# Gate and up's tiles 8 and 9: the fourth block product by seven products in half-width banks instead of by two plain ones

## The chip, the cores and the metric

The kernel runs on one core of one Trainium2 chip. The metric is the device time of one execution in microseconds; lower is better. The profile comes from one further execution, with TensorE (PE), its weight loads (PEld), VectorE (DVE), ScalarE (ACT), GpSimd (POOL) and SyncE (SP, which issues most transfers) recorded apart.

## The reference, cut to what matters

```python
xn = _layernorm(x, axis=-1)                       # x: 8 x 1024 x 512, f32
s = _L0_attn_ref(xn, Wq, Wk, Wv, Wo, Wg, decay_logits, out_scale)
# _L0_ffn_ref, with INTER = 1376 rows of gate and up, weights looked up in a table of 16
gate = einsum('bsh,oh->bso', xn, lut[gate_idx])
up = einsum('bsh,oh->bso', xn, lut[up_idx])
h = silu(gate) * up
ffn = einsum('bsh,oh->bso', h, lut[down_idx])
x = x + s * silu(ffn)
```

The change touches only `gate` and `up`, for 256 of the 1376 rows (tiles 8 and 9 of 128 rows each; tile 10 has the 96 left over).

## The kernel before, in words

A first phase does the attention for all eight batch entries (bodies) and builds the weights of the feed-forward part, which it writes to DRAM. A second phase does gate, up and down body by body, 1024 tokens each. All in float32. `keep_order` pins the instructions of TensorE, VectorE, ScalarE and GpSimd to the order in which the program was traced, so that each engine's queue is what the code says, line after line.

Gate and up are computed by a Strassen-like scheme on two levels. On the outer level, a 2 x 2 block product is done by seven block products, named by the keys 1 to 7. Of each tile's weights the blocks and their sums lie in `W_OF` order, of x in `X_OF` order. On the inner level, each block product is again done by seven products, by the same scheme, for which x has seven halves of columns (`H` = 256 tokens) in `D_OF` order; `sums_of_x` makes them in place, so that one raw quarter of x is overwritten and has to be fetched again by `restore` before the raw blocks are used.

A `Node` is one step of the inner level. It holds four PSUM banks of 512 columns, in the roles s11, s12, s21 and sE, of which there are two each, and has two halves, `a` = 0 and 1, each of 256 columns. Its seven products each issue two matmuls of 256 columns, one per half:

- `first`: product 1 into s11, and ScalarE copies s11 to s12 (L794).
- `fifth` and `fifth_copy`: product 5 into sE, and ScalarE copies it to `e` in SBUF (L801).
- `sixth`: product 6 onto s12; ScalarE copies s12 to s21 (L805); VectorE adds `e` to s12 (L806).
- product 2 onto s11. Then s11 is complete: quarter 0.
- `seventh`: product 7 onto s21; VectorE writes s21 + `e` to sE (L810), which is quarter 3.
- product 3 onto s12 (quarter 1), and product 4 onto s21 (quarter 2).

As a quarter gets complete, the step's `empty(t, n)` brings it out of PSUM. The loop in `quads` interleaves two nodes: the following node's product 1 goes between the node's products 2 and 7, and the following node's product 5 between products 3 and 4.

For the tiles 0 to 7 a node's two halves are two pairs of tiles with one key (`steps(q)` for q = 0 and 1, of `NQ` = 2). For the one pair left, tiles 8 and 9 (q = `NQ`), the two halves are two keys: (1, 6), (5, 7), (2, 3), by `pair_steps`. `node_23` ends with two VectorE additions (L924, L926) and two silus on ScalarE (L925, L927) for each quarter. Key 4 is left over. It is done by the class `Fourth`: each of the two tiles has one product of 512 columns by the plain scheme, of two matmuls (L826) from the raw blocks of x, which VectorE adds to `u3` (L835). `Fourth` stands in the loop as the following of node (2, 3): its first product lies between that node's products 2 and 7, its second between products 3 and 4. After it, `after_23` multiplies both halves of h by u3 and e5 on GpSimd (L936).

Next comes, in the bodies 1 to 7, tile 10 by `single` (the tail o = 10, seven products of two 512-column matmuls, L731, from raw blocks of x); in body 0 that tile was done ahead of the quads. Then `down` runs with its own nodes (`DownNode`, L1037 to L1075; its copies are L1059, L1066 and L1070).

Weights come through `ring`, three slots, one per node, `Fourth` or tail; SP issues a node's load as soon as the slot of three nodes earlier is free.

The restores of x are issued from ScalarE's queue (L853): (4) by the last node of quad 1, and after that (1, 6), (5, 7) and (2, 3) by the pair's nodes.

Of the kernel before, what the change touches and what calls it, by code (L numbers as in the profile page):

```python
# [9 lines left out]
F32 = mybir.dt.float32  # L10
# [4 lines left out]
ALU = mybir.AluOpType  # L15
AX = mybir.AxisListType

P = 128
# [30 lines left out]
def recurrent_block(ctx: ExitStack, tc, x, wq, wk, wv, wo, wg, decay_logits, out_scale, lut, gidx, uidx, didx, out):  # L49
# [19 lines left out]
    nc = tc.nc  # L69
# [5 lines left out]
    U = 512  # L75
# [5 lines left out]
    NK = (NO - 1) // 2  # L81
# [164 lines left out]
    def ffn_weights(build, pool, pair_pool):  # L246
# [9 lines left out]
        def gate_up(o):  # L256
            s, m = OCH[o]
            n = 2 * NV * m
            idx = build.tile([P, NB], I32, name="idx", tag="idx", bufs=2)
            iv = idx[:, :n].rearrange("p (a b) -> p a b", b=m)  # L260
            gs, us = (src[:, s : s + m].rearrange("(c p) b -> p c b", p=P) for src in (gidx, uidx))
            nc.sync.dma_start(out=iv[:, 2:6, :], in_=gs)
            nc.sync.dma_start(out=iv[:, 0:2, :], in_=us[:, 0:2, :])
            nc.sync.dma_start(out=iv[:, 6:8, :], in_=us[:, 2:4, :])
            yield
            wf = pool.tile([P, 2 * NB], F32, name="wgu", tag="wgu", bufs=2)
            yield from look_up(build, wf[:, :n], idx[:, :n], P, n)
            w = wf[:, : 2 * n].rearrange("p (k two m) -> p k two m", two=2, m=m)
            a21, a11, a12, a22, s1, s2, s3, s4 = (w[:, k] for k in range(8))
            nc.gpsimd.tensor_tensor(s1, a21, a22, ALU.add)  # L270
            nc.gpsimd.tensor_tensor(s2, s1, a11, ALU.subtract)
            yield
            nc.gpsimd.tensor_tensor(s3, a11, a21, ALU.subtract)
            nc.gpsimd.tensor_tensor(s4, a12, s2, ALU.subtract)
            wide = wf[:, 2 * m : 2 * n].rearrange("p (a b) -> p a b", b=m)
            if o >= 4 * NQ:
                defer(3, lambda: nc.sync.dma_start(out=wgu_d[o], in_=wide))
            if o >= 2 * NK:
                return
            if o % 2 == 0:  # L280
                upper.append(w[:, 1:])
                return
            up, low = upper.pop(), w[:, 1:]
            to = quad_d[o // 4][:, :, o // 2 % 2, :].rearrange("p k (t m) -> p k t m", m=P)
            pair = pair_pool.tile([P, 7, 4, P], F32, name="pair", tag="pair")
            nc.sync.dma_start(out=to[:, :, 0:2, :], in_=up)
            defer(3, lambda: nc.sync.dma_start(out=to[:, :, 2, :], in_=low[:, :, 1, :]))
            b21, b22, b11, b12 = low[:, :, 0], low[:, :, 1], up[:, :, 0], up[:, :, 1]
            nc.gpsimd.tensor_tensor(pair[:, :, 0], b21, b22, ALU.add)
            yield  # L290
            nc.gpsimd.tensor_tensor(pair[:, :, 1], pair[:, :, 0], b11, ALU.subtract)
            yield
            nc.gpsimd.tensor_tensor(pair[:, :, 2], b11, b21, ALU.subtract)
            yield
            nc.gpsimd.tensor_tensor(pair[:, :, 3], b12, pair[:, :, 1], ALU.subtract)
            defer(4, lambda: nc.sync.dma_start(out=to[:, :, 3:7, :], in_=pair))
            for _ in range(3):
                yield
# [383 lines left out]
    def phase_2():  # L682
        with (
# [12 lines left out]
            def bank(role, name):  # L696
                return psp.tile([P, U], F32, name=name, tag=role)
# [62 lines left out]
            class Node:  # L760
# [2 lines left out]

                def __init__(self, b, q, ks, xs):
                    self.ks, self.xs = ks, xs

                    self.restores = ks if q == NQ else (4,) if (q, ks) == (NQ - 1, (4, 4)) else ()
                    name = f"{b}_{q}_{ks[0]}"  # L770
                    self.w = ring.tile([P, 2, 7, P], F32, name=f"wq{name}", tag="wr")
                    w = self.w.rearrange("p a t m -> p a (t m)")
                    if q < NQ:
                        nc.sync.dma_start(out=w, in_=quad_d[q][:, W_OF[ks[0]], :, :])
                    else:
                        for a, k in enumerate(ks):
                            nc.sync.dma_start(out=w[:, a, :], in_=quad_d[q][:, W_OF[k], 0, :])
                    self.t = [bank(r, f"{r}{name}") for r in ("s11", "s12", "s21", "sE")]
                    self.name = f"e{name}"

                def product(self, n, i, start=False):
                    for a in range(2):
                        nc.tensor.matmul(  # L783
                            self.t[n][:, ts(a, H)],
                            lhsT=self.w[:, a, (0, 1, 6, 2, 3, 4, 5)[i - 1], :],
                            rhs=self.xs[:, X_OF[self.ks[a]], D_OF[i], :],
                            start=start and a == 0,
                            stop=False,
                            skip_group_check=True,
                        )  # L790

                def first(self):
                    self.product(0, 1, True)
                    nc.scalar.copy(self.t[1], self.t[0])  # L794

                def fifth(self):
                    self.product(3, 5, True)
                    self.e = tmp.tile([P, U], F32, name=self.name, tag="e")

                def fifth_copy(self):  # L800
                    nc.scalar.copy(self.e, self.t[3])  # L801
# [6 lines left out]
                def seventh(self):  # L808
                    self.product(2, 7)
                    nc.vector.tensor_tensor(self.t[3], self.t[2], self.e, ALU.add)  # L810

            class Fourth:


                def __init__(self, b, xs, u3):
                    self.b, self.xs, self.u3 = b, xs, u3
                    self.w = ring.tile([P, 14, P], F32, name=f"w4{b}", tag="wr")
                    for r in range(2):
                        nc.sync.dma_start(
                            out=self.w[:, ts(r, 2), :], in_=wgu_d[4 * NQ + r][:, ts(W_OF[4], 2), :]  # L820
                        )

                def product(self, r, role):
                    ps = bank(role, f"{role}{self.b}_4_{r}")
                    for n in range(2):
                        nc.tensor.matmul(  # L826
                            ps,
                            lhsT=self.w[:, 2 * r + n, :],
                            rhs=self.xs[:, X_OF[4], ts(n, 2), :],
                            start=n == 0,  # L830
                            stop=n == 1,
                            skip_group_check=True,
                        )
                    o = self.u3[:, ts(r, 2), :]
                    return lambda: nc.vector.tensor_tensor(o, ps.rearrange("p (a t) -> p a t", a=2), o, ALU.add)  # L835

                def first(self):
                    self.product(0, "s11")()

                def fifth(self):  # L840
                    self.add = self.product(1, "sE")

                def fifth_copy(self):
                    self.add()

            def quads(b, xs, h, sums, at_last):

# [53 lines left out]
                def pair_steps():  # L901
# [2 lines left out]
                        (t[:, :, :H], t[:, :, H:])  # L904
                        for t in (tmp.tile([P, 4, U], F32, name=f"{k}{b}_l", tag=k) for k in ("p1", "u2"))
                    )
                    room[0] = u3

                    def of_h(half, n):
                        r, c = divmod(n, 2)  # L910
                        t = half * U + c * H
                        return h[:, 4 * NQ + r, t : t + H]
# [10 lines left out]
                    def node_23(t, n):  # L923
# [2 lines left out]
                        nc.vector.tensor_tensor(of_h(1, n), t[n][:, H:], u2[:, n], ALU.add)  # L926
                        nc.scalar.activation(of_h(1, n), of_h(1, n), AF.Silu)  # L927

                    def after_57():
                        for n in (0, 3, 1, 2):  # L930
                            nc.gpsimd.tensor_tensor(e5[:, n], e5[:, n], u3[:, n], ALU.add)

                    def after_23():
                        for half, other in ((0, u3), (1, e5)):
                            for n in (0, 3, 1, 2):
                                nc.gpsimd.tensor_tensor(of_h(half, n), of_h(half, n), other[:, n], ALU.mult)  # L936

                    yield (1, 6), node_16, None
                    yield (5, 7), node_57, after_57
                    yield (2, 3), node_23, after_23  # L940

                room = [None]
                def every():
                    for q in range(NQ):
                        for ks, empty, after in steps(q):
                            yield Node(b, q, ks, xs), empty, after
                    for ks, empty, after in pair_steps():
                        yield Node(b, NQ, ks, xs), empty, after
                    yield Fourth(b, xs, room[0]), None, None
                    yield None, None, None  # L950

                todo = every()
# [381 lines left out]
```

## Time and profile before

| | us |
|---|---|
| median of 3 runs | 2119.15 (2118.79 to 2119.32) |
| profiled execution, its time | 2119.36 |
| its span, first to last instruction | 2117.6 |
| TensorE busy | 2109.2 |
| VectorE busy | 1409.2 |
| GpSimd busy | 1021.2 |
| ScalarE busy | 929.4 |
| matmuls of Fourth (L826), 64 records, busy | 30.0 |

The granted TensorE clock is 1.000. A matmul in float32 shows as two records. Its recorded duration is longer than its share of the pipeline (592 ns for a record of 512 columns, 379 ns for 256), since successive matmuls overlap: the pace is read from the starts. In the timeline a row begins with its start and its duration in microseconds; xN at the end merges N instructions, and the bracket gives the idle time of the engine before it and what ended that.

### The profile page before, as it was taken

Reading aid. Unit: us, or ns where it says so; the run is one execution under the profiler, and the core shown is the slowest. Engines: PE = TensorE matmul, PEld = TensorE weight load, DVE = VectorE, ACT = ScalarE, POOL = GpSimd, SP = SyncE. Lnnn points to the kernel's source line nnn. Section 1 sums busy time; section 2 is a strip of 40 time slices with the busy share of each in tenths; the row PEclk is TensorE's granted clock in tenths of the full one; section 3 lists DMA queues with packets and bytes.
Section 4 is the critical chain, followed back from the end, with each engine's and each line's share of the span. In section 5 each row is a group of like instructions: output and inputs, shape, how many; then the busy total and the mean of one; then the engine's idle time right before and its main releaser. Section 6 shows DMA issues by size and latency. Waiting matters only on the chain.

```text
span 2117.6 us, 31134 instructions
## 1 busy us (share of the span) xinstructions
PE 2109.2 (100%) x11306; PEld 1678.6 (79%) x11306; DVE 1409.2 (67%) x2150; ACT 929.4 (44%) x2083; POOL 1021.2 (48%) x1046
## 2 busy tenths in 40 slices
PE   9999999999999999999999999999999999999999
PEld 6666666666678888887879888887978888797877
DVE  6889888678545774576567556656755665675557
ACT  3666666666434414423441442344145324423531
POOL 2554565253354537416642752655275255527432
PEclk9999999999999999999999999999999999999999
DMA  7556557565464644464455446444544634464442
GB/s 195 158 176 160 190 174 169 181 129 177 110 252 153 240 168 153 156 236 140 146 195 185 151 148 245 139 147 172 208 151 154 246 123 155 165 218 148 152 154 109
DMA packets 164271, 361.45 MB, mean 171 GB/s; under 512 B 52083, under 2 KB 90230, under 8 KB 163094
## 3 DMA queue, kind: packets, MB, share of 16 engines
q1 hardware_dynamic: 149702, 336.12, 48.7%
q0 software_dynamic: 4480, 14.68, 1.7%
q10 hardware_dynamic: 9936, 8.66, 1.4%
q8 instruction: 90, 1.47, 0.3%
q14 instruction: 63, 0.52, 0.1%
HBM read 282.87 MB, written 76.55 MB: 170 GB/s over the span
## 4 chain that ended last, share of the span: by engine, by line
PE 98%; DVE 1%; DMA 1%; POOL 0%; issue 0%; ACTq 0%; ACT 0%; SPq 0%; POOLq 0%; DVEq 0%
PE s L783 33%; PE pq L455 10%; PE pv L418 8%; PE sE L783 6%; PE s12d L1037 5%; PE s21d L1037 5%; PE s11d L1037 5%; PE po L583 4%; PE fs L731 3%; PE pd L1145 3%; PE ps L1152 3%; PE sEd L1037 2%; PE psc L561 2%; PE pu L569 2%; PE pt L411 1%; PE fsE L731 1%
## 5 line engine op out<-in xcount | busy, mean ns | idle before, releaser
L783 PE MATMUL s<-xs,wq 128*128 128x256 f32 x3264 | 731.2, 379 | 0.0
L783 PEld LDWEIGHTS s<-xs,wq 128*128 128x128 f32 x3264 | 619.6, 190 | 95.8 <-issue 8.1
L806 DVE TENSOR_TENSOR s<-s,e 128x512 f32<-128x512 f32 x136 | 95.1, 699 | 204.1 <-ACT s L805 204.0
L455 PE MATMUL pq<-xnT,wqk_sb 128*128 128x512 f32 x512 | 230.3, 592 | 0.0
L1116 POOL TENSOR_TENSOR cu<-cu 128x256 f32<-128x256 f32 x32 | 34.8, 1088 | 306.7 <-DVE cl L1115 306.7
L418 PE MATMUL pv<-wvg_sb,xnT 128*128 128x387 f32 x512 | 177.6, 489 | 0.3 <-DMA wvg_sb<-in_wv 0.3
L714 POOL TENSOR_TENSOR xs<-xs 128x256 f32<-128x256 f32 x224 | 170.8, 789 | 4.5
L455 PEld LDWEIGHTS pq<-xnT,wqk_sb 128*128 128x128 f32 x512 | 92.4, 190 | 92.1 <-issue 91.8
L810 DVE TENSOR_TENSOR sE<-s,e 128x512 f32<-128x512 f32 x136 | 95.0, 699 | 104.9 <-PE s L783 104.9
L874 POOL TENSOR_TENSOR u<-u,e 128x512 f32<-128x512 f32 x64 | 79.9, 1270 | 148.7 <-DVE u L870 130.2
L801 ACT COPY e<-sE 128x512 f32<-128x512 f32 x136 | 79.6, 585 | 138.8 <-PE sE L783 138.5
L783 PE MATMUL sE<-xs,wq 128*128 128x256 f32 x544 | 139.6, 379 | 0.0
L397 POOL TENSOR_SCALAR rstd<-rstd 128x1 f32<-128x1 f32 x56 | 27.8, 497 | 229.6 <-ACT junk L396 229.0
L418 PEld LDWEIGHTS pv<-wvg_sb,xnT 128*128 128x128 f32 x512 | 92.7, 190 | 54.8 <-issue 2.4
L878 POOL TENSOR_TENSOR h<-h,u 128x512 f32<-128x512 f32 x64 | 80.1, 1272 | 113.1 <-DVE u L885 103.5
L794 ACT COPY s<-s 128x512 f32<-128x512 f32 x136 | 77.5, 570 | 109.2 <-PE s L783 105.1
L805 ACT COPY s<-s 128x512 f32<-128x512 f32 x136 | 77.5, 570 | 97.6 <-PE s L783 97.6
L1037 PE MATMUL s12d<-wdd,z 128*128 128x128 f32 x896 | 118.5, 275 | 0.6 <-ACT s12d L1059 0.6
L783 PEld LDWEIGHTS sE<-xs,wq 128*128 128x128 f32 x544 | 103.4, 190 | 14.0
L1037 PEld LDWEIGHTS s12d<-wdd,z 128*128 128x128 f32 x896 | 109.1, 192 | 0.8 <-ACT s12d L1059 0.8
L224 DVE TENSOR_SCALAR leaf<-idx,lut_x,lut_sb 128x1024 int32<-128x1024 int32 (+2 forms) x119 | 101.3, 876 | 0.0
L563 DVE TENSOR_TENSOR pr<-psc,w_tab 128x384 f32<-128x384 f32 x64 | 35.5, 555 | 92.0 <-PE psc L561 91.8
(236 smaller groups left out, 4254.3 us busy)
## 6 DMA issues: line engine op xcount, KB each, us to landing
wq<-quadd SPq DMA_DIRECT2D x112, 896.0 KB, 4.5
wdd<-wdd SPq DMA_DIRECT2D x56, 896.0 KB, 4.8
xs<-xsd SPq DMA_DIRECT2D x56, 512.0 KB, 6.6
wq<-quadd SPq DMA_DIRECT2D x48, 448.0 KB, 4.1
x<-in_x SPq DMA_DIRECT2D x64, 256.0 KB, 5.9
xsd<-ts SPq DMA_DIRECT2D x8, 2048.0 KB, 7.5
gx<-in_x SPq DMA_DIRECT2D x64, 256.0 KB, 5.4
out<-gx POOLq DMA_DIRECT2D x56, 256.0 KB, 2.3
```

Of the source, the lines that this page charges most:

```text
L224: nc.vector.tensor_scalar(o.bitcast(I32), iv, lut_x[:rows, k, :], lut_i[:rows, k, 0:1], ALU.bitwise_and, ALU.bitwise_xor,)
L418: nc.tensor.matmul(pv, lhsT=xnT[:, v, ts(c, P)], rhs=wvg_sb[:, v, :], start=(v == 0), stop=(v == NV - 1))
L455: nc.tensor.matmul(pq, lhsT=wqk_sb[:, v, ts(j, D)], rhs=xnT[:, v, ts(hf, U)], start=(v == 0), stop=(v == NV - 1))
L583: nc.tensor.matmul(po, lhsT=lh, rhs=rh, start=(n == 0), stop=(n == len(prods) - 1))
L714: nc.gpsimd.tensor_tensor(o, x1, x2, ALU.subtract)
L731: nc.tensor.matmul(ps, lhsT=w[:, 2 * W_OF[k] + n, :m], rhs=xs[:, X_OF[k], 2 * n : 2 * n + 2, :], start=start and n == 0, stop=stop and n == 1,
L783: nc.tensor.matmul(self.t[n][:, ts(a, H)], lhsT=self.w[:, a, (0, 1, 6, 2, 3, 4, 5)[i - 1], :], rhs=self.xs[:, X_OF[self.ks[a]], D_OF[i], : ...
L806: nc.vector.tensor_tensor(self.t[1], self.t[1], self.e, ALU.add)
L810: nc.vector.tensor_tensor(self.t[3], self.t[2], self.e, ALU.add)
L874: nc.gpsimd.tensor_tensor(o[:, n], o[:, n], other[:, n], ALU.add)
L878: nc.gpsimd.tensor_tensor(of_h(half, n), of_h(half, n), two(other[:, n]), ALU.mult)
L1037: nc.tensor.matmul(self.t[n][:, ts(a, P)], lhsT=self.lhs[i][:, e, ts(a, P)], rhs=self.w[:, e, D_OF[i], :], start=start and a == 0 and e == ...
```

## The change

`Fourth` goes. Its place is taken by a fourth node of the pair's steps, with the keys (4,): a `Node` with a single half, so that each of its seven products is one matmul of 256 columns into the left of its bank, and its copies and sums have 256 columns. The loop is not changed, so that the node's products 1 and 5 lie where Fourth's two products were, and its products 6, 2, 7, 3 and 4 follow node (2, 3)'s product 4. Its quarters are added to u3 one by one on VectorE (`node_4l`), and the multiplication of the first half of h by u3 moves behind it; that of the second half by e5 stays after node (2, 3). Its weights are those of the inner level, 896 columns of one key in one load, and so the plain weights of tiles 8 and 9 are no longer written in the first phase. The restore of key 4 moves from quad 1's last node to the new one, since Fourth's raw blocks are not needed any more.

```diff
--- before.py
+++ after.py
@@ -273,7 +273,7 @@
             nc.gpsimd.tensor_tensor(s3, a11, a21, ALU.subtract)
             nc.gpsimd.tensor_tensor(s4, a12, s2, ALU.subtract)
             wide = wf[:, 2 * m : 2 * n].rearrange("p (a b) -> p a b", b=m)
-            if o >= 4 * NQ:
+            if o >= 2 * NK:
                 defer(3, lambda: nc.sync.dma_start(out=wgu_d[o], in_=wide))
             if o >= 2 * NK:
                 return
@@ -763,10 +763,11 @@
 
 
 
+
                 def __init__(self, b, q, ks, xs):
                     self.ks, self.xs = ks, xs
 
-                    self.restores = ks if q == NQ else (4,) if (q, ks) == (NQ - 1, (4, 4)) else ()
+                    self.restores = ks if q == NQ else ()
                     name = f"{b}_{q}_{ks[0]}"
                     self.w = ring.tile([P, 2, 7, P], F32, name=f"wq{name}", tag="wr")
                     w = self.w.rearrange("p a t m -> p a (t m)")
@@ -775,11 +776,12 @@
                     else:
                         for a, k in enumerate(ks):
                             nc.sync.dma_start(out=w[:, a, :], in_=quad_d[q][:, W_OF[k], 0, :])
-                    self.t = [bank(r, f"{r}{name}") for r in ("s11", "s12", "s21", "sE")]
+                    self.n = len(ks) * H
+                    self.t = [bank(r, f"{r}{name}")[:, : self.n] for r in ("s11", "s12", "s21", "sE")]
                     self.name = f"e{name}"
 
                 def product(self, n, i, start=False):
-                    for a in range(2):
+                    for a in range(len(self.ks)):
                         nc.tensor.matmul(
                             self.t[n][:, ts(a, H)],
                             lhsT=self.w[:, a, (0, 1, 6, 2, 3, 4, 5)[i - 1], :],
@@ -795,7 +797,7 @@
 
                 def fifth(self):
                     self.product(3, 5, True)
-                    self.e = tmp.tile([P, U], F32, name=self.name, tag="e")
+                    self.e = tmp.tile([P, U], F32, name=self.name, tag="e")[:, : self.n]
 
                 def fifth_copy(self):
                     nc.scalar.copy(self.e, self.t[3])
@@ -808,40 +810,6 @@
                 def seventh(self):
                     self.product(2, 7)
                     nc.vector.tensor_tensor(self.t[3], self.t[2], self.e, ALU.add)
-
-            class Fourth:
-
-
-                def __init__(self, b, xs, u3):
-                    self.b, self.xs, self.u3 = b, xs, u3
-                    self.w = ring.tile([P, 14, P], F32, name=f"w4{b}", tag="wr")
-                    for r in range(2):
-                        nc.sync.dma_start(
-                            out=self.w[:, ts(r, 2), :], in_=wgu_d[4 * NQ + r][:, ts(W_OF[4], 2), :]
-                        )
-
-                def product(self, r, role):
-                    ps = bank(role, f"{role}{self.b}_4_{r}")
-                    for n in range(2):
-                        nc.tensor.matmul(
-                            ps,
-                            lhsT=self.w[:, 2 * r + n, :],
-                            rhs=self.xs[:, X_OF[4], ts(n, 2), :],
-                            start=n == 0,
-                            stop=n == 1,
-                            skip_group_check=True,
-                        )
-                    o = self.u3[:, ts(r, 2), :]
-                    return lambda: nc.vector.tensor_tensor(o, ps.rearrange("p (a t) -> p a t", a=2), o, ALU.add)
-
-                def first(self):
-                    self.product(0, "s11")()
-
-                def fifth(self):
-                    self.add = self.product(1, "sE")
-
-                def fifth_copy(self):
-                    self.add()
 
             def quads(b, xs, h, sums, at_last):
 
@@ -904,8 +872,6 @@
                         (t[:, :, :H], t[:, :, H:])
                         for t in (tmp.tile([P, 4, U], F32, name=f"{k}{b}_l", tag=k) for k in ("p1", "u2"))
                     )
-                    room[0] = u3
-
                     def of_h(half, n):
                         r, c = divmod(n, 2)
                         t = half * U + c * H
@@ -926,27 +892,31 @@
                         nc.vector.tensor_tensor(of_h(1, n), t[n][:, H:], u2[:, n], ALU.add)
                         nc.scalar.activation(of_h(1, n), of_h(1, n), AF.Silu)
 
+                    def multiply_by(half, other):
+                        for n in (0, 3, 1, 2):
+                            nc.gpsimd.tensor_tensor(of_h(half, n), of_h(half, n), other[:, n], ALU.mult)
+
                     def after_57():
                         for n in (0, 3, 1, 2):
                             nc.gpsimd.tensor_tensor(e5[:, n], e5[:, n], u3[:, n], ALU.add)
 
                     def after_23():
-                        for half, other in ((0, u3), (1, e5)):
-                            for n in (0, 3, 1, 2):
-                                nc.gpsimd.tensor_tensor(of_h(half, n), of_h(half, n), other[:, n], ALU.mult)
+                        multiply_by(1, e5)
+
+                    def node_4l(t, n):
+                        nc.vector.tensor_tensor(u3[:, n], t[n], u3[:, n], ALU.add)
 
                     yield (1, 6), node_16, None
                     yield (5, 7), node_57, after_57
                     yield (2, 3), node_23, after_23
-
-                room = [None]
+                    yield (4,), node_4l, lambda: multiply_by(0, u3)
+
                 def every():
                     for q in range(NQ):
                         for ks, empty, after in steps(q):
                             yield Node(b, q, ks, xs), empty, after
                     for ks, empty, after in pair_steps():
                         yield Node(b, NQ, ks, xs), empty, after
-                    yield Fourth(b, xs, room[0]), None, None
                     yield None, None, None
 
                 todo = every()
```

On each engine the order is otherwise the same. On ScalarE the node's three copies and restores come in between node (2, 3)'s silus in this order: silus of quarter 0, copy to s12, silus of quarters 3 and 1, copy of e, restore of (2, 3), silus of quarter 2, copy to s21, restore of (4). The line numbers of the changed kernel are other ones: L785 for the products, L796, L803, L807 for ScalarE's copies, L808 and L812 for VectorE's sums, L821 for restores, L890 to L893 for node (2, 3), L897 for the multiplications and L907 for the additions to u3.

## The prediction

> **What bounds the kernel now.** I read the page first: its busy shares, its granted clock and its chain of waits.
>
> ```profile
> PE 2109.2 (100%) x11306; PEld 1678.6 (79%) x11306; DVE 1409.2 (67%) x2150; ACT 929.4 (44%) x2083; POOL 1021.2 (48%) x1046
> ...
> PEclk9999999999999999999999999999999999999999
> ...
> PE 98%; DVE 1%; DMA 1%; POOL 0%; issue 0%; ACTq 0%; ACT 0%; SPq 0%; POOLq 0%; DVEq 0%
> ```
>
> TensorE is busy in 2109.2 of 2117.6 us, at full clock. Its waits confirm this: without the start-up, the longest is one of 0.6 us in the whole span. So a matmul taken out is a gain in full, and a wait put on TensorE is a loss in full; VectorE at 67% and ScalarE at 44% do not bound by amount, only by being late. The next view is the timeline around the changed place in body 1, from the last product of node (5,7) to the tail o = 10:
>
> ```profile
> 1080.23 2.75 PE L783 MATMUL s<-xs,wq 128*128 128x256 f32 x12
> ...
> 1082.21 0.57 ACT L805 COPY s<-s 128x512 f32<-128x512 f32 x1 [0.55 <-PE s L783]
> 1082.82 0.70 DVE L806 TENSOR_TENSOR s<-s,e 128x512 f32<-128x512 f32 x1 [0.69 <-ACT s L805]
> 1082.82 1.88 PE L826 MATMUL s<-xs,w 128*128 128x512 f32 x4
> ...
> 1084.54 1.89 PE L783 MATMUL s<-xs,wq 128*128 128x256 f32 x8
> ...
> 1086.26 1.88 PE L826 MATMUL sE<-xs,w 128*128 128x512 f32 x4
> ...
> 1087.98 1.03 PE L783 MATMUL s<-xs,wq 128*128 128x256 f32 x4
> ...
> 1089.05 0.42 DVE L924 TENSOR_TENSOR p_l<-s,p_l 128x256 f32<-128x256 f32 x1
> ...
> 1089.39 0.41 DVE L926 TENSOR_TENSOR h<-s,p_l 128x256 f32<-128x256 f32 x1
> 1089.50 0.42 ACT L925 ACTIVATE h<-p_l 128x256 f32<-128x256 f32 x1 [1.29 <-DVE p_l L924]
> 1089.83 0.42 ACT L927 ACTIVATE h<-h 128x256 f32<-128x256 f32 x1
> ```
>
> Every matmul is two records. Starts tell the pace: from 1082.82 to 1084.54 four records of 512 columns take 1.72 us, 0.43 us each, and from 1084.54 to 1086.26 eight of 256 columns take the same, 0.215 each. So a 512-column matmul costs 0.86 us and a 256-column one 0.43 us. Also read here: an engine that empties a bank starts 0.21 us after the product's last slot (1087.98 + 0.86 + 0.21 = 1089.05), and the last of node (2,3)'s silus ends at 1090.25, 2.27 us after that node's fourth product (key 4) began. That delay matters to nobody today, since ScalarE's next copy waits for the tail's first product. The third view is the same place in body 0, where no tail follows and the down node starts at once:
>
> ```profile
> 724.23 0.42 ACT L925 ACTIVATE h<-p_l 128x256 f32<-128x256 f32 x1 [1.11 <-DVE p_l L924]
> ...
> 724.56 0.42 ACT L927 ACTIVATE h<-h 128x256 f32<-128x256 f32 x1
> 724.89 0.37 ACT L1059 COPY s12d<-s11d 128x256 f32<-128x256 f32 x1
> 725.30 1.16 PE L1037 MATMUL s12d<-wdd,z 128*128 128x128 f32 x8 [0.61 <-ACT s12d L1059]
> ```
>
> A copy from one bank to the next stands in ScalarE's queue behind the last silus, and TensorE waits for it. It restarts 0.04 us after the copy's end, and the eight records take until 726.30, 1.00 us instead of the 0.89 of the eight before: 0.1 us of restart.
>
> **The change: matmuls.** Each body loses Fourth's four 512-column matmuls, 4 x 0.86 = 3.44 us, and gets seven of 256 columns, 7 x 0.43 = 3.01. That is 0.43 us less, 3.4 us over eight bodies, all on the path.
>
> **Where they stand.** In before, Fourth's two products are filler in node (2,3)'s iteration, after its second and its third product, and nothing depends on them soon. Now node (4,) leaves two single matmuls there (products 1 and 5), and the five others follow node (2,3)'s fourth product in a row: 6, 2, 7, 3, 4, at 0.43 us each, with no following node between them. Call the start of that fourth product S; it ends at S+0.86, then 6 starts at +0.86, 2 at +1.29, 7 at +1.72, and the tail would begin at +3.01.
>
> Node (2,3) itself still fits. Its copy L805 ends 2.55 us after the start of (5,7)'s fourth product, and product 7 is due at 3.01; its sE sum (L810) ends about 0.39 us ahead of S. With the shorter filler these margins are 0.46 and 0.39 us, and I cost them at nothing; without them each body would pay what is missing.
>
> **The new wait.** Product 7 of node (4,) accumulates onto the copy of product 6's bank (now L807), and in ScalarE's order that copy stands behind: four silus of quarters 3 and 1, the copy of e (now L803), the issue of the restore for (2,3), and the two silus of quarter 2. Quarter 2 can be added only after S+0.86+0.21 = +1.07; the two adds run +1.07 to 1.48 and +1.40 to 1.81 (starts 0.33 apart in the rows above). Quarter 1 is emptied by +1.05, its silus end at +1.51, and the e copy runs +1.43 to 1.80. The issue of the restore takes 0.37 us (+1.50 to 1.87; the row of L853 has 0.37). The silus of quarter 2 run +1.90 to 2.32 and +2.23 to 2.65, the copy +2.57 to 2.93 (0.357 by L1070). Product 7 starts at +2.97 instead of +1.72: 1.25 us of wait, 0.1 of restart. VectorE adds e to the copied bank in +2.97 to 3.40 (0.43, L1071), so product 3 goes at once, +3.50 to 3.93. The sum of product 7 with e starts at +3.50+0.21 = 3.71 and ends at 4.13; product 4 writes the bank it reads, and so starts at +4.17, with 0.1 of restart, and ends at +4.70. The tail starts at +4.70, not +3.01: 1.69 us of waits, less the 0.43 saved, is about **+1.25 us per body**, +8.75 for bodies 1 to 7.
>
> In body 0 VectorE also does the first sums for down between these steps (0.68 to 1.37 us each), so quarter 2 is added later: with (5,7)'s fourth product at 714.13 I get the copy's end at 722.75, product 7 at 722.79 and the first down product at about 724.97, against 722.74 before. But the down node's own wait (0.61 + 0.1) goes, since the silus are past by then: its sixth product starts at 724.97 + 1.80 = 726.77, against 725.40 with its restart counted: +1.4. What is late next is the down node's own chain of banks, as before.
>
> **What lies beside it.** ScalarE gets three copies of 0.36 a body, VectorE six operations of 0.42 for two of 0.69: hidden by their idle shares but for the waits named. Bounds for the restore's issue between two ScalarE operations: 0.13 us late (issue after the copy's dispatch, taken), nothing, or 0.37. The block-4 restore moves from quad 1 into ScalarE's queue behind L807, where it waits for product 7; the operation after it is the tail's first copy, due 1.9 us after the tail starts. It lands in 2.8 us (at most 6.5), and the tail's product 4 is last, some 10 us later: nothing. On POOL the four products with u3 go behind the four with e5 and wait for the new node; 4 x 0.73 us after the last add they are done, beside 12 us of tail; in body 0 the first down product that reads them is some 4 us off. Were that cover gone, POOL's last 1.5 us would show. On SP, two writes of 917 KB leave the first phase and sixteen loads of 131 KB the second; eight loads of 459 KB come. Issued like Fourth's at 1075.24, one lands in 4.1 us by the row of 448 KB, 3.4 us before its first use at 1082.8. Nothing.
>
> **A rule against it.** The row of 0.61 us in body 0 shows that TensorE's clock survives a short gap: the 0.89 us pace returns with the next eight records, and PEclk is 9 everywhere. The Trainium skill, page "TensorE: Matmul & The Clock Gate", section "A second HAM failure mode: psum-queue depth-cycling", says that short idles between groups of matmuls that cycle through banks can make the clock swing to half; its Part 1 gives the window as about 3.4 us. By that rule each body could run one window at half pace, an estimate of 1.7 us, 13.6 in all; by the row it costs 0. I take the row: two gaps of 1.25 and 0.24 us per body are nearer to it than to a sequence of bursts.
>
> **The sum.** 8.75 + 1.4 = 10.15 us on the profiled execution (span 2117.6, time 2119.36, 0.2 above the median 2119.15). On the median: 2129.3.
>
> **The rivals.** (A) The waits are hidden, and the saving stands: 3.4 us, plus the 0.7 to 0.9 of body 0's old wait that goes, -3.4 to -4.3, 2115 to 2115.7. Mechanism: the copy of product 6's bank is in time. It decides at S+1.72 for no wait and at about +2.15 for break-even on the first wait alone, against my +2.93; that would need the two silus of quarter 2 and the restore's issue out of the way. For it: ScalarE is only 44% busy. Against it: its queue is in order, and the body-0 row is that very wait. (B) Waits of the same kind but smaller: the issue hidden (-0.13), no restart (-0.2): +0.92 a body, +7.3, 2126.5. Or larger: the issue added in full (+0.24) and some 0.1 more at semaphores: +1.6 a body, +12.8, 2132. (C) The clock swings: 10.15 + 13.6, about 2143. (D) The change does not do what it says: half-width matmuls could cost as much as wide ones, which would turn the saving into a loss; the 256-column rows at 0.215 exclude it.
>
> **How the numbers follow.** My forecast with (B)'s both ends has 0.85; A 0.07; C 0.03; 0.05 lies between A and the low end, where part of the wait is covered. The range goes from 2122, some way into that gap, to 2134, a little above the high end of (B). About 0.2% (4.2 us) is what a measurement here can tell. A lies nearly all within it, so faster is 0.02, same 0.09, slower 0.89.
>
> **What would show it.** The profile after should have a wait of TensorE for L807 of some 1.2 us in each of eight bodies, one of 0.2 for L812, the body-0 wait for the down copy gone, the 256-column pace at 0.215 and PEclk at 9. It is wrong if TensorE's waits total under 8 us, if product 7 starts within 2.2 us of S, or if matmuls after the wait are slow.

## The result: 0.44% slower, for the waits that were forecast

The changed kernel takes 2128.2 us in the median of six runs (2127.7 to 2130.3), before takes 2118.9 (2118.8 to 2119.3): +9.3 us, a ratio of 1.0044 with the interval 1.0034 to 1.0055. 2129.3 had been forecast, in the range 2122 to 2134. The profiled execution has a span of 2125.9 us where before has 2117.6, so +8.3.

The page of the changed kernel, busy time and clock:

```profile
PE 2110.3 (99%) x11354; PEld 1685.3 (79%) x11354; DVE 1415.6 (67%) x2182; ACT 936.0 (44%) x2107; POOL 1015.2 (48%) x1046
...
PEclk9999999999999999999999999999999999999999
```

TensorE is no longer busy all the time, at an unchanged clock. What it waits for, by the view of its waits (total in us, times, longest):

```profile
PE s L785 <- ACT s L807: 7.2, 8, 1.4
PE warm L359 <- POOL nhalf L148: 1.4, 1, 1.4
PE s L785 <- DVE s L808: 0.6, 1, 0.6
...
PE s L785 <- DVE sE L812: 0.4, 1, 0.4
```

L807 is the copy of node (4,)'s product 6, once in each of eight bodies; before has no such row. The down node's wait for its own copy (0.61 us) is gone. The place in body 1, from the timeline:

```profile
1087.43 1.89 PE L785 MATMUL s<-xs,wq 128*128 128x256 f32 x8
...
1088.49 0.42 DVE L890 TENSOR_TENSOR p_l<-s,p_l 128x256 f32<-128x256 f32 x1
...
1088.61 0.37 ACTq L821 DMA_DIRECT2D xs<-xsd  x1
1088.84 0.41 DVE L892 TENSOR_TENSOR h<-s,p_l 128x256 f32<-128x256 f32 x1
1088.84 0.35 ACT L803 COPY e<-sE 128x256 f32<-128x256 f32 x1
1089.10 0.42 ACT L891 ACTIVATE h<-p_l 128x256 f32<-128x256 f32 x1
1089.41 0.41 ACT L893 ACTIVATE h<-h 128x256 f32<-128x256 f32 x1
1089.72 0.37 ACT L807 COPY s<-s 128x256 f32<-128x256 f32 x1
1090.12 0.43 DVE L808 TENSOR_TENSOR s<-s,e 128x256 f32<-128x256 f32 x1 [0.88 <-ACT s L807]
...
1090.14 1.92 PE L785 MATMUL s<-xs,wq 128*128 128x256 f32 x6 [0.83 <-ACT s L807]
...
1090.88 0.43 DVE L812 TENSOR_TENSOR sE<-s,e 128x256 f32<-128x256 f32 x1
...
1091.37 0.30 PEld L785 LDWEIGHTS s<-xs,wq 128*128 128x128 f32 x2 [0.46 <-DVE sE L812]
...
1091.91 3.60 PE L731 MATMUL fs<-xs,wr 128*96 128x512 f32 x8
```

S, the start of node (2,3)'s product 4, is 1087.43. Eight records (that product, then node (4,)'s 6 and 2) fill the time to 1089.15. ScalarE goes on without a hole through copy of e, two silus and L807, and TensorE starts product 7 at 1090.14, 0.05 us after L807 ends: 0.99 us late. (The row says 0.83 because a record's modelled end lies beyond its slot.) Three matmuls later the tail starts at 1091.91; without waits these take 1.29 us, so another 0.48 us went: L812 ends at 1091.31 and product 4 starts at 1091.37, 0.22 us late by the starts of single records, and most of the rest are two restarts of 0.10 us, behind either wait. (The view of waits counts from modelled ends, and so lists L812 for body 0 alone.)

The cleanest measure is the time of a whole body: TensorE is in order and full, so the first quad product of one body and of the next give it. From the timelines, body 1 of before and of the changed kernel:

```profile
794.30 1.03 PE L783 MATMUL s<-xs,wq 128*128 128x256 f32 x4
...
982.59 0.59 PE L783 MATMUL s<-xs,wq 128*128 128x256 f32 x2
```

```profile
795.29 1.03 PE L785 MATMUL s<-xs,wq 128*128 128x256 f32 x4
...
984.61 0.59 PE L785 MATMUL s<-xs,wq 128*128 128x256 f32 x2
```

188.29 us became 189.32, and the next five pairs of starts give 189.33 each: +1.04. Body 0 went from 177.85 to 179.34, +1.49. The last body, taken to the end of the span, went from 193.54 to 194.66, +1.12. Together that is 8.8 to 8.9; the first quad began 0.5 us earlier (615.95 against 616.45), which leaves the 8.3 of the spans. The first phase's end differed by up to 0.9 us between all profiles here (615.84 to 616.77), so 0.5 us is no effect of the change that could be told.

### The profile page after: what moved, and what is told of

Read it like the earlier page. It is cut to its first block, busy times and chain, and to the rows that moved or that the text cites. A ratio compares the mean times of both kernels' runs of the same rounds, so it can differ in the third digit from the quotient of the medians.

```text
span 2125.9 us, 31296 instructions
## 1 busy us (share of the span) xinstructions
PE 2110.3 (99%) x11354; PEld 1685.3 (79%) x11354; DVE 1415.6 (67%) x2182; ACT 936.0 (44%) x2107; POOL 1015.2 (48%) x1046
## 4 chain that ended last, share of the span: by engine, by line
PE 97%; DVE 1%; ACT 1%; issue 0%; DMA 0%; POOL 0%; ACTq 0%; SPq 0%; POOLq 0%; DVEq 0%
PE s L785 33%; PE pq L455 10%; PE pv L418 8%; PE sE L785 6%; PE s12d L1007 5%; PE s21d L1007 5%; PE s11d L1007 5%; PE po L583 4%; PE fs L731 3%; PE pd L1115 3%; PE ps L1122 3%; PE sEd L1007 2%; PE psc L561 2%; PE pu L569 2%; PE pt L411 1%; PE fsE L731 1%
## 5 line engine op out<-in xcount | busy, mean ns | idle before, releaser
L785 PE MATMUL s<-xs,wq 128*128 128x256 f32 x3360 | 755.5, 380 | 8.6 <-ACT s L807 7.2
L785 PEld LDWEIGHTS s<-xs,wq 128*128 128x128 f32 x3360 | 635.7, 190 | 107.3 <-ACT s L807 10.4
L808 DVE TENSOR_TENSOR s<-s,e 128x512 f32<-128x512 f32 x144 | 98.6, 684 | 210.2 <-ACT s L807 210.1
L812 DVE TENSOR_TENSOR sE<-s,e 128x512 f32<-128x512 f32 x144 | 98.6, 684 | 105.9 <-PE s L785 104.8
L785 PE MATMUL sE<-xs,wq 128*128 128x256 f32 x560 | 144.4, 379 | 0.0
L803 ACT COPY e<-sE 128x512 f32<-128x512 f32 x144 | 82.5, 573 | 139.0 <-PE sE L785 136.7
L796 ACT COPY s<-s 128x512 f32<-128x512 f32 x144 | 80.5, 559 | 109.2 <-PE s L785 105.2
L807 ACT COPY s<-s 128x512 f32<-128x512 f32 x144 | 80.5, 559 | 97.2 <-PE s L785 97.1
L785 PEld LDWEIGHTS sE<-xs,wq 128*128 128x128 f32 x560 | 106.4, 190 | 14.5
```

What stands on the lines that cost most here:

```text
L785: nc.tensor.matmul(self.t[n][:, ts(a, H)], lhsT=self.w[:, a, (0, 1, 6, 2, 3, 4, 5)[i - 1], :], rhs=self.xs[:, X_OF[self.ks[a]], D_OF[i], : ...
L808: nc.vector.tensor_tensor(self.t[1], self.t[1], self.e, ALU.add)
```

## The experiments

Body times below are read in the same way, from one profile each; the ratios are to runs of before on the same chip.

| | time, us | before, us | ratio (interval) | body 0 | bodies 1 on |
|---|---|---|---|---|---|
| before | | | | 177.85 | 188.29 |
| changed | 2128.2 | 2118.9 | 1.0044 (1.0034 to 1.0055) | 179.34 | 189.33 |
| e1_silus_behind | 2124.9 | 2119.3 | 1.0024 (1.0014 to 1.0033) | 179.34 | 188.71 |
| e3_tail_between | 2119.4 | 2119.3 | 1.0000 (0.9991 to 1.0008) | 179.34 | 187.88 |
| e4_node4_ahead | 2125.4 | 2119.3 | 1.0029 (1.0017 to 1.0041) | 178.76 | 188.7 to 189.1 |
| e5_restore_later | 2128.5 | 2119.3 | 1.0042 (1.0027 to 1.0057) | 179.34 | 189.33 |
| e7_sums_behind | 2126.2 | 2119.4 | 1.0033 (1.0019 to 1.0046) | 177.59 | 189.33 |
| e6_all_between | 2116.5 | 2119.4 | 0.9986 (0.9980 to 0.9993) | 177.75 | 187.88 |
| e8_sums_spread | 2115.2 | 2119.4 | 0.9980 (0.9973 to 0.9988) | 177.10 | mostly 187.88 |

**e1_silus_behind: is it the place in ScalarE's queue?** In `node_23` the silus of quarter 2 are put off, and with them the multiplications by e5; in the loop they come behind `sixth`:

```diff
+                        def silus():
+                            nc.scalar.activation(of_h(0, n), p1[:, n], AF.Silu)
+                            nc.scalar.activation(of_h(1, n), of_h(1, n), AF.Silu)
...
                     node.sixth()
+                    while pending:
+                        pending.pop(0)()
```

> The changed kernel with one alteration: the two silus of node (2,3)'s quarter 2, and the multiplications of the second half of h with e5, are traced behind the copy of node (4,)'s product 6 (L807) instead of ahead of it. Same instructions, same TensorE order. Theory (the copy is late because ScalarE's in-order queue has those silus ahead of it): the copy runs at about S+1.75 instead of S+2.29, product 7 waits about 0.4 us instead of 0.99, the second wait (product 4 for the sum of product 7 with e) grows to about 0.25 to 0.35, and each of bodies 1 to 7 gains about 0.6 us: some 4 us faster than the changed kernel, about 2123.5 to 2124, still some 5 us slower than before. Rival (half-width steps of 0.43 us are too short for a copy and a sum between them, whatever else is queued): the copy's place makes no difference, within 1 us of the changed kernel.

Bodies 1 on fell by 0.62 us, where 0.6 was expected. The timeline of its body 1 (S at 1087.22) has the copy at S+1.66 instead of S+2.29, right behind the copy of e, and product 7 at S+2.09, 0.37 us late:

```profile
1088.63 0.35 ACT L803 COPY e<-sE 128x256 f32<-128x256 f32 x1
1088.88 0.38 ACT L807 COPY s<-s 128x256 f32<-128x256 f32 x1
1089.18 0.41 ACT L894 ACTIVATE h<-p_l 128x256 f32<-128x256 f32 x1
...
1089.31 1.92 PE L785 MATMUL s<-xs,wq 128*128 128x256 f32 x6 [0.21 <-ACT s L807]
```

So most of the first wait was the silus' place. The second wait, expected to grow, stays at 0.22 us. What is left, +0.42 us a body over before, belongs to the chain itself: even with nothing but the copy of e ahead, copy and sums don't fit into steps of 0.43 us. Both readings hold a part, the silus the larger one. Body 0 gains nothing: there the wait only moves from L807 to VectorE's sum L808, for 1.6 us, which e7 takes up.

**e3_tail_between: does the node save its 0.43 us when its waits are covered?** `single` becomes a generator that stops around its first two products, and the loop runs these as it runs a following node's:

```diff
-                    yield None, None, None
+                    yield tail and Ahead(tail), None, None
...
+                yield
                 product(pa, 1, True, False)
                 nc.scalar.copy(u2, pa)
+                yield
                 product(pb, 6, True, True)
                 nc.vector.tensor_tensor(u2, pb, u2, ALU.add)
+                yield
```

> The changed kernel, in bodies 1 to 7 with the tail's first product (two 512-column matmuls) between node (4,)'s products 2 and 7, and its second between products 3 and 4; ScalarE's and VectorE's queues keep their order but for the tail's own two operations. Body 0 is as in the changed kernel. Theory (the node's arithmetic is cheaper, and only the waits cost): both waits are covered by 1.72 us of the tail's matmuls, bodies 1 to 7 lose 1.04 + 0.43 us each against the changed kernel, 10.3 us in all: about 2117.5 to 2118, some 1 us faster than before, and that although body 0 still pays its 2 us. Rival (clock, weight loads or contention cost what the waits were blamed for): the time stays more than 3 us above before although the waits of TensorE for L807 are gone.

Bodies 1 on take 187.88 us, 0.41 less than before and 1.45 less than in the changed kernel. The same copy (L810 here) is as late as before, and nobody waits for it, as the timeline of body 1 shows:

```profile
1087.90 1.88 PE L731 MATMUL fs<-xs,wr 128*96 128x512 f32 x4
...
1088.46 0.37 ACT L810 COPY s<-s 128x256 f32<-128x256 f32 x1
...
1089.62 1.03 PE L788 MATMUL s<-xs,wq 128*128 128x256 f32 x4
```

The copy ends at 1088.83, product 7 comes at 1089.62 behind the tail's product. That settles that the arithmetic is cheaper by what was counted, 0.41 us where 0.43 were reckoned, and leaves no more than that difference for clock, weight loads and new transfers. The whole time stands level with before: the expected gain of some 1 us is inside its interval, and body 0 still pays.

**e4_node4_ahead: the other order.** The two `yield` lines of nodes (2,3) and (4,) are exchanged, and the multiplication by u3 goes to `after_23`.

```diff
+                    yield (4,), node_4l, None
                     yield (2, 3), node_23, after_23
-                    yield (4,), node_4l, lambda: multiply_by(0, u3)
```

> The changed kernel with node (4,) ahead of node (2,3), so that node (2,3)'s full-width products 1 and 5 are the filler between node (4,)'s steps, and node (2,3) is the last with nothing between its steps. Theory: no wait in node (4,); in node (2,3), with 0.86 us a step, the copy of product 6 is just in time and product 4 waits 0.3 to 0.4 us for the sum, since two additions of quarter 0 stand ahead of it on VectorE. Bodies 1 to 7 gain about 1.1 us each against the changed kernel, 7.5 us; body 0 gains nothing, as its down node again waits for silus: about 2120 to 2121, 1 to 2 us slower than before. Rival (any seven-product node without a following node costs a wait of about 1 us or more, whatever its width): no gain of more than 3 us.

A miss in size: 3.5 us better than the changed kernel by the bodies of the profiles, 2.9 by the medians, but no 7.5. Of the 3.5, 0.6 come in body 0, for which nothing was expected. The rival's line of 3 us lies between the two, so the time doesn't decide; the timeline does. Up to the tail's start body 1 comes out as in before (14.65 us from the fourth product of node (1,6), 1075.04 to 1089.69; 1074.19 to 1088.84 in before), so the saving of 0.43 and the missing filler of node (2,3) cancel, nearly as reckoned: a full-width node without filler costs some 0.4 us, not 1. What was overlooked is in its waits:

```profile
PE fs L731 <- DMA xs<-xsd: 2.5, 8, 0.5
```

The restore of (2,3) now stands behind the late silus on ScalarE's queue and is issued at 1090.22, after the tail has begun, and the tail's fourth product, of key 2, waits for it in the bodies 1 to 7: 2.3 of those 2.5 us, as 0.2 are at the start in before too. By the starts it is 0.4 to 0.65 us a body, nearly all by which these bodies exceed before; only body 4 waits 0.3 us for L807 besides.

**e5_restore_later: what does an issue on ScalarE's queue cost?**

```diff
                     node.sixth()
+                    if node.ks == (4,):
+                        restore(2, 3)
...
-                    if node.restores:
+                    if node.restores and node.ks != (2, 3):
```

> The changed kernel with the restore of (2,3) issued from ScalarE behind the copy of node (4,)'s product 6 (L807) instead of between the copy of e and the silus of quarter 2. It measures one term of the prediction's sum: the issue was put at 0.13 us between two operations. By that term: about 0.13 us a body, 1.0 us in all. Rival (the issue runs ahead on the sequencer while ScalarE is still busy, as the changed kernel's timeline has it at S+1.18, and costs nothing): within 0.3 us of the changed kernel, and the copy at S+2.29 as before.

Nothing: the bodies take 189.33 and 179.34 us as in the changed kernel. The issue overlaps with the operation still running, as in the timeline above, where it starts at 1088.61, ahead of the copy of e that precedes it in the queue.

**e7_sums_behind: body 0's extra wait.** Only the calls of `at_last` change, which have an effect in body 0 alone:

```diff
-                    at_last(node.ks == (2, 3))
                     node.seventh()
...
-                    at_last(node.ks in ((5, 7), (2, 3)))
+                    at_last(node.ks == (5, 7))
                     if following:
...
-                    at_last(node.ks in ((5, 7), (2, 3)))
+                    at_last({(5, 7): 1, (4,): 3}.get(node.ks, 0))
                     if after:
```

> The changed kernel with only body 0 altered: the three first sums for down that VectorE does during node (2,3) are moved behind node (4,)'s additions. Bodies 1 to 7 have no such sums and stay at 189.33 us each. Theory (in body 0 those sums delay quarter 2's additions, the silus behind them and the sum of e, and so add about 1.3 us of waits to those of the other bodies): the wait for L807 falls from 1.44 us to about 0.83 as in the other bodies, the waits for L808 and for L812 ahead of node (2,3)'s product 4 go, and body 0 falls by 1.5 to 2 us: about 1.8 us faster than the changed kernel. Rival (the sums only move, and the down node waits for them instead): body 0 stays within 0.5 us of 179.34.

Body 0 falls by 1.75 us to 177.59, 0.26 less than in before, and bodies 1 on stay at 189.33. So what body 0 paid for the new node was the place of those sums. The longest wait for L807 falls from 1.4 to 0.8 us, and those that the view listed for L808 and L812 are gone. Little of it comes back: the second down node starts 0.13 us late for a sum. The row of L807 is now:

```profile
PE s L785 <- ACT s L807: 6.6, 8, 0.8
```

**e6_all_between: both covers.** e3, e7's `at_last`, and in body 0 the first `DownNode` as the following of node (4,):

```diff
+                    if b:
+                        return Ahead(tail)
+                    first_down = DownNode(b, 1, blocks(h)[0], got[0])
+                    return first_down
```

> The tail's first two products between node (4,)'s steps as in e3_tail_between, and in body 0 the first down node's products 1 and 5 there, with the three first sums for down, which VectorE did during node (2,3), moved behind node (4,)'s additions. Theory: every body now keeps the saving of 0.43 us; the bodies 1 to 7 take 0.41 us less than before each, as in e3; body 0 loses the 1.49 us that it pays in the changed kernel and, since the down node's old wait for its copy (0.61) and for a sum (0.39) goes too, ends up some 1.6 us below before, the copy's wait in node (4,) shrinking to about 0.1 us. Sum: 2.9 + 1.6 = 4.5 us less than before, about 0.2% faster (2114.5 where before has 2119). Rival (body 0's extra time was VectorE's amount of work, not its place): body 0 stays at +1 us or more, and the gain over before is under 2.5 us.

Faster than before by 0.14%, by 2.9 us where 4.5 were expected. What is missing is missing in body 0 alone: 177.75 us, not 176.3. There the wait for the copy is gone, but the sums are now late for the second down node:

```profile
PE s11d L1024 <- DVE sx L992: 1.3, 1, 1.3
```

Neither reading was right in full: the place matters, and the new place was too late.

**e8_sums_spread: the same sums one by one.** One behind quarter 2 of node (2,3), one behind quarter 1 of node (4,), one behind its quarter 2. Against e6:

```diff
-                    at_last(node.ks == (5, 7))
+                    at_last(node.ks in ((5, 7), (4,)))
                     if following:
...
-                    at_last({(5, 7): 1, (4,): 3}.get(node.ks, 0))
+                    at_last(node.ks in ((5, 7), (2, 3), (4,)))
```

> As e6_all_between, with the three first sums for down in body 0 spread: one behind node (2,3)'s quarter-2 additions, one behind node (4,)'s quarter-1 addition, one behind its quarter-2 addition. In e6 all three stood in a row ahead of the sum that the second down node's first product reads, and TensorE waited 1.34 us for it. Theory (VectorE has holes of about 0.9 us beside the copy of product 6 that take a sum for nothing): that wait goes, the others stay away, and body 0 falls from 177.75 us to about 176.4; bodies 1 to 7 stay at 187.88. About 1.3 us faster than e6, 4.3 us or 0.2% faster than before. Rival (VectorE is behind by then whatever the order): the wait for the sum stays above 0.8 us or comes back as a wait for node (4,)'s sums, and body 0 stays above 177.3.

2115.2 us, 0.2% faster than before: like e6, it beats both kernels. Body 0 falls to 177.10, not to 176.4, for the wait for the sum made room for another:

```profile
PE s11d L1024 <- DMA wdd<-wdd: 0.7, 1, 0.7
```

The second down node's weights, loaded into the slot that node (2,3) frees, land late for a body that has got shorter. In two of the later bodies (188.17 and 188.25 us) the tail's weights, too, land late for its earlier start, by 0.24 and 0.30 us. So the bodies of e8 add up to what those of e6 do, and the 1.4 us between the two medians are no gain that the profiles show. Body 0's gain of 0.75 us over before is not all the new node's: whether before, too, would gain from the down node's products as filler was not tried.

## Why the prediction was right, step by step

- **The saving of 0.43 us a body.** Right: 0.41 in e3, once nothing waits.
- **Node (2,3) with the shorter filler costs nothing.** Right for seven bodies: the changed kernel has no TensorE wait ahead of S in bodies 1 to 7. In body 0 there was one, 0.35 us for L812, since a sum for down took 1.18 us instead of 0.68 and stood ahead of it.
- **The copy behind the silus, +1.25 us a body.** Right in kind, e1 shows it; 1.04 in size. Product 7 was put at S+2.97 and came at S+2.71. Half of that is the issue of the restore: 0.13 us assumed between two ScalarE operations, 0 in e5. The rest is spacing: the first silu of quarter 2 starts 0.26 us after the copy of e, and the next two operations follow at 0.31 us each, where about 0.34 had been taken. The second wait with the restarts was put at 0.44 us and measured 0.48.
- **Body 0, +1.4 us.** 1.49 in the profile, but by luck: two errors cancel. The first down product came 11.63 us after node (5,7)'s fourth, not 10.84. Of these 0.79 us, 0.47 are there at product 7, behind the wait for L812 above; 0.32 come after it, since the last sum took 1.77 us, not 1.37, and product 3 waited 0.61 us for L808. Against it, a wait of before that the prediction had not counted went, worth 0.66 us by the starts with its restart:

```profile
735.79 0.71 PE L1048 MATMUL s11d<-wdl,sx 128*128 128x128 f32 x4 [0.39 <-DVE sx L1005]
```

- **The sum.** 7 x 1.04 + 1.49 = 8.8 us against 10.15. The medians, 9.3 apart, lie nearer to the forecast than the bodies do. The signs of being wrong stayed away, the first one narrowly: the view's waits for L807, L808 and L812 make 8.2 us, where under 8 was the sign; product 7 came at S+2.71, not within 2.2.
- **Clock.** Gaps of 0.99 and some 0.2 us in each body leave the granted clock where it was (0.999 in the profile, 1.000 before) and the pace at 0.215 us a record, so the price of the swings (13.6 us) wasn't paid.
- **The rivals.** Of (B) one half came true, the hidden issue; the restarts, which it left out, stayed at 0.10 us. The copy in time, on which (A) rests, is what e3 makes true by other means.
- **Weights, transfers and POOL at nothing.** Right: no wait of TensorE for a weight load or a product on GpSimd appears in the changed kernel behind its start-up.

## What to carry to other kernels

Fewer multiply cycles by a deeper scheme means a chain: product, copy, product, sum. On a TensorE that was as full as here, such a node paid only where other matmuls lay between its steps (-0.41 us a body in e3, +1.04 without them); half as wide, it needs them more, as each step covers half the time. Before adding one, look for what the evacuating engine has in its queue ahead of the copy, and put an independent product, here the next block's first one, into each place where the chain turns.

## What the runs showed of the hardware that was not expected

- A transfer's issue in ScalarE's queue took 0.37 us in the records and cost nothing between two operations: it started 0.23 us ahead of the copy before it in the order (1088.61 and 1088.84), and its removal from there changed no body by more than 0.01 us.
- Where no transfer came late, body times repeat to 0.01 us within a profile and between profiles: 189.33 in the changed kernel, e5 and e7, 187.88 in e6 and in all but one body of e3 (187.96). Where one did, they don't: 188.73 to 189.05 in e4. Differences of 0.03% a body could so be read from one profile, while the times of whole runs spread by 2 to 3 us.
- VectorE's same sum for down (128x512, both operands in SBUF) took 0.68 us or up to 1.22 us, in both kernels. In the profile of before, the 176 of these 256 sums with no GpSimd operation beside them took 0.67 to 0.69 us each, and all 40 above 0.76 us had one beside them. In body 0 of the changed kernel the sum of 1.18 us lay beside a GpSimd addition that also took 1.18 us, where its neighbours took 0.73. That GpSimd's work is the cause was not tried.
